# Graph layer with relation weights: statistics of three node blocks moved to ScalarE, the first line's cell columns to VectorE, scatters and first-edge loads reordered

## The chip, the cores and the metric

One core of one Trainium2 chip runs the whole program. The metric is device time in microseconds (us) of one execution. The core has TensorE (PE, matmuls), VectorE (DVE), ScalarE (ACT), GpSimd (POOL) and SyncE (SP, which issues most plain DMAs). Each engine executes its own queue strictly in order and waits there on semaphores of others. GpSimd issues the indirect DMAs (gathers and scatters); in the profile such a DMA keeps POOL busy for about a microsecond.

## The reference

```python
h = relu(layernorm(x))                         # x: 625 x 512
for r in range(4):                             # 20625 edges, sorted by dst
    total_msg += (h[src] @ W_rel[r] + b_rel[r]) * where(edge_type == r, edge_weight, 0)[:, None]
agg = segment_sum(total_msg, dst) / maximum(segment_sum(edge_weight, dst), 1)[:, None]
x1  = layer_norm(h + h @ W_self + b_self + agg, ln1_g, ln1_b)
out = x + layer_norm(x1 + gelu(x1 @ W_ffn1 + b_ffn1) @ W_ffn2 + b_ffn2, ln2_g, ln2_b)
```

## The kernel before

The 625 nodes lie in NB = 5 blocks of up to 128 rows. The program has three stages.

**Table stage.** For each of the R = 4 relations and each block, one step (20 steps, `step = r * NB + i`) multiplies the normalised block with the relation's weights (`table_rows`, L463), VectorE adds the bias and scales the rows (L476), and SP stores them in a DRAM table of 4 x 640 rows. A message of an edge is then one row of that table times the edge's weight. `pre_norm` prepares a block: mean and variance on VectorE (L437, L439), `z = relu(x - mean)` on VectorE for blocks 0 to 2 (L427) and on ScalarE for blocks 3 and 4 (L424), and `(var + eps) ** -0.5` on GpSimd (`rsqrt_pow`, L399), which `table_rows` uses as the rows' scale. PE then transposes z (L406) and ScalarE copies the result (L412). During the first relation, the transposes of block i + 1 stand between the second and third matmul of block i.

In the same 20 steps the edges are prepared. The edges of the first and last node block are not gathered by row: GpSimd scatters their weights into a matrix of "cells" in DRAM (L746), 46 columns of 128 edges each, in two "lines" (31 columns of block 0, 15 of block 4). `line_columns` computes keys and places for a whole line, `line_sums` (L732 to L740) then handles a piece of up to 8 columns on VectorE, and each column becomes one `scatter`: an indirect DMA and a small memset (L749). `load_sums` brings a finished cell matrix back to SBUF; chunk sums (L1485) multiply it with the table. For the inner blocks, `first_edges` finds on PE and VectorE the first edge group of each node (`x_group`, L906), GpSimd loads three tiles of them (`x_edges`, L910), and `first_rows` on VectorE turns these into table rows. Tuples such as `COLUMNS_AT` say at which step each of these parts is written.

**Edge stage.** GpSimd gathers 102 tiles of 128 table rows (L1308, three of them at L1386), each into one of 10 buffers `ms`. ScalarE and VectorE weigh or add them and split them into a high and a low part (`eh`, `el`), and PE sums them by node with one-hot matrices (L1369). Chunk sums, self parts (L501), layer norms and the feed-forward products (L1054, L1074) of finished blocks fill the other engines. The order of this stage is written out as a list of operation numbers, `ORDER`, which was fitted beforehand with a model of durations and due times; each engine then runs it in order. The first gather stands behind a small memset that waits until all but the last table row block are stored (`after_stores`, L761).

**Tail.** The last block's sums, norm, feed-forward and store.

Of the kernel before, what the change touches and what calls it, by code (L numbers as in the profile page):

```python
# [16 lines left out]
P = 128  # L17
# [7 lines left out]
class EdgePlan:  # L25
# [176 lines left out]
def gnn_layer(ctx, tc, x, edges, edge_line, edge_groups, w_self, w_rel, w_ffn1, w_ffn2, rows_in, bf_in, out, n_edges):  # L202
# [218 lines left out]
    def pre_norm(i, mean):  # L421
        if i > 2:
            nc.scalar.activation(rx[:, i, 2:3], mean, AF.Copy, scale=-1.0)
            nc.scalar.activation(z[:, i, :], xs[:, i, :], AF.Relu, bias=rx[:, i, 2:3])  # L424
        else:
            for c in (slice(0, D // 2), slice(D // 2, D)) if i == 0 else (slice(0, D),):
                nc.vector.tensor_scalar(z[:, i, c], xs[:, i, c], mean, 0.0, op0=ALU.subtract, op1=ALU.max)  # L427
# [752 lines left out]
    with tc.manual_schedule(engines={PE, DVE, ACT, mybir.EngineType.Pool}):  # L1180
# [12 lines left out]
        for r in range(R):  # L1193
            for i in range(NB):
# [8 lines left out]
                if step + 3 < NB:  # L1203
                    pre_norm(step + 3, x_stats(step + 3))
# [560 lines left out]
```

## Time and profile before

| | us |
|---|---|
| median of 3 runs | 260.82 (260.43 to 260.83) |
| the profiled execution, its own time | 259.69 |
| its span | 257.8 |
| busy: PE, DVE, POOL, ACT | 241.5, 198.6, 169.3, 106.4 |

The profiled execution is 1.13 us faster than the median of the runs, and 1.9 us of its time lie outside the span. A timeline row reads: start, duration, engine, line, operation, output <- inputs, and in square brackets how long the engine had been idle before it and what ended that. `x4` is a merged run of four; a 128 x 512 float32 matmul appears as two records, so the four matmuls of a step give eight.

### The profile page before, as it was taken

To read this page: it belongs to the slowest core of one execution; us is meant where nothing else is said; L and a number is where in the kernel's file an instruction comes from. 1 tells how busy PE (TensorE), PEld (TensorE's weight loads), DVE (VectorE), ACT (ScalarE), POOL (GpSimd) and SP (SyncE) were. 2 spreads that over 40 slices of the span, in tenths; PEclk is the share of its full clock that TensorE was granted. 3 is DMA by queue.
4 is the path that set the end of the run, shared out by engine and by line. 5 is a ranking of instruction groups with operands and counts; after the bars stand their busy time and mean duration, and the time that the engine had idled before them with its cause. 6 is when DMAs were issued, how large, how long until landed. Compare 5 with 4: busy or idle time off the path is not lost.

```text
span 257.8 us, 3594 instructions
## 1 busy us (share of the span) xinstructions
PE 241.5 (94%) x1051; PEld 141.5 (55%) x1051; DVE 198.6 (77%) x474; ACT 106.4 (41%) x328; POOL 169.3 (66%) x230
## 2 busy tenths in 40 slices
PE   8899999999999958899999999999999999999980
PEld 6334444344455623455544466657966759549660
DVE  2787799998999750999867999898887897764344
ACT  3036600000231011876544655695666664606420
POOL 5487888688875867777777777778777777410000
PEclk9999999999999995999999999999999999999997
DMA  6999999983371149979889998776777677501021
GB/s 188 334 396 410 383 368 368 299 328 133 95 275 43 45 135 402 355 211 336 256 285 354 367 342 267 214 215 188 207 211 214 213 218 215 182 0 43 0 84 40
DMA packets 23997, 59.44 MB, mean 231 GB/s; under 512 B 4419, under 2 KB 8743, under 8 KB 22822
## 3 DMA queue, kind: packets, MB, share of 16 engines
q0 software_dynamic: 9728, 26.79, 33.6%
q1 hardware_dynamic: 13920, 30.91, 33.3%
q10 hardware_dynamic: 326, 1.48, 1.6%
q8 instruction: 9, 0.15, 0.2%
q14 instruction: 14, 0.11, 0.1%
HBM read 49.99 MB, written 9.17 MB: 229 GB/s over the span
## 4 chain that ended last, share of the span: by engine, by line
PE 64%; DVE 13%; DMA 10%; ACT 4%; POOL 4%; issue 3%; SPq 1%; POOLq 0%; DVEq 0%
PE ps L463 16%; PE ps L1054 11%; PE ps L1074 11%; PE acc L1485 10%; PE acc L1369 8%; PE ps L501 4%; DMA tr<-table 3%; DMA line<-in_edge_line_dram 2%; DMA out_dram<-ow 2%; DMA ms<-table,row_i 2%; POOL cells L746 2%; POOL x_edges L910 1%; DVE ow L1099 1%; PE ps L673 1%; PE ps L406 1%
## 5 line engine op out<-in xcount | busy, mean ns | idle before, releaser
L1308 POOL DMA_INDIRECT ms<-table,row_i x99 | 97.1, 981 | 31.2 <-issue 16.0
L463 PE MATMUL ps<-wr,T 128*128 128x512 f32 (+2 forms) x168 | 71.3, 577 | 0.8 <-ACT T L412 0.8
L746 POOL DMA_INDIRECT cells<-weight,cell x46 | 47.7, 1036 | 10.7 <-issue 6.4
L463 PEld LDWEIGHTS ps<-wr,T 128*128 128x128 f32 x168 | 30.4, 190 | 35.7 <-issue 29.2
L1344 DVE SCALAR_TENSOR_TENSOR add<-ms,wgt_g,add 128x512 f32<-128x512 f32 x55 | 40.4, 749 | 6.7 <-ACT add L1314 3.5
L1054 PEld LDWEIGHTS ps<-T,w_sb 128*128 128x128 f32 x320 | 39.2, 191 | 5.9 <-issue 3.3
L1054 PE MATMUL ps<-T,w_sb 128*128 128x128 f32 (+2 forms) x320 | 39.8, 275 | 0.5 <-ACT T L1548 0.4
L1074 PE MATMUL ps<-w_sb,gT 128*128 128x512 f32 (+2 forms) x96 | 36.5, 523 | 0.3 <-ACT gT L1060 0.3
L1485 PE MATMUL acc<-tr,sums_w 128*128 128x512 f32 x60 | 31.2, 623 | 0.5 <-DMA tr<-table 0.5
L1314 ACT ACTIVATE add<-ms,wgt_g 128x512 f32<-128x512 f32 x30 | 20.6, 688 | 10.7 <-DVE el L1322 8.9
L1074 PEld LDWEIGHTS ps<-w_sb,gT 128*128 128x128 f32 x96 | 16.6, 190 | 13.6 <-issue 9.3
L1318 ACT CAST eh<-add 128x512 fp32r<-128x512 f32 x25 | 14.5, 583 | 15.1 <-DVE add L1344 14.0
L1322 DVE TENSOR_TENSOR el<-add,eh 128x512 fp32r<-128x512 f32 x25 | 17.0, 683 | 3.4 <-ACT eh L1318 1.8
L1369 PE MATMUL acc<-eh,oh 128*128 128x512 f32 x34 | 16.3, 511 | 3.3 <-ACT eh L1332 3.3
L501 PE MATMUL ps<-ws_sb,T 128*128 128x512 f32 x40 | 18.6, 592 | 0.0
L659 ACT ACTIVATE ohw<-os,w 128x128 fp32r<-128x128 f32 x34 | 10.7, 389 | 18.0 <-DVE os L641 18.0
L1060 ACT ACTIVATE gT<-ps,bf 128x128 f32<-128x128 f32 (+1 forms) x40 | 13.6, 359 | 11.0 <-PE ps L1054 10.6
L1369 PE MATMUL acc<-el,oh 128*128 128x512 f32 x34 | 16.7, 516 | 1.2 <-DVE el L1336 0.7
L1485 PEld LDWEIGHTS acc<-tr,sums_w 128*128 128x128 f32 x60 | 10.8, 194 | 8.1 <-issue 5.5
L1332 ACT ACTIVATE eh<-ms,ed 128x512 fp32r<-128x512 f32 x9 | 6.2, 712 | 21.1 <-DMA tr<-table 15.8
L476 DVE SCALAR_TENSOR_TENSOR tr<-ps,rx,brel_bc 128x512 f32<-128x512 f32 x15 | 11.1, 743 | 4.8 <-PE ps L463 4.8
L1336 DVE SCALAR_TENSOR_TENSOR el<-ms,ed,eh 128x512 fp32r<-128x512 f32 x9 | 6.6, 747 | 9.1 <-ACT eh L1332 9.1
(250 smaller groups left out, 314.8 us busy)
## 6 DMA issues: line engine op xcount, KB each, us to landing
tr<-table SPq DMA_DIRECT2D x11, 512.0 KB, 5.8
w_sb<-in_L_gnn_W_ffn_dram SPq DMA_DIRECT2D x2, 2048.0 KB, 10.0
table<-tr SPq DMA_DIRECT2D x15, 256.0 KB, 4.4
wr<-in_L_gnn_W_rel_dram SPq DMA_DIRECT2D x3, 1024.0 KB, 7.8
cells<-zeros SPq DMA_DIRECT2D x2, 1280.0 KB, 10.8
ms<-table,row_i POOLq DMA_INDIRECT x99, 3.9
rows<-in_rows_dram SPq DMA_DIRECT2D x1, 1280.0 KB, 12.7
sums_w<-cells ACTq DMA_DIRECT2D x1, 1280.0 KB
```

What stands on the lines that cost most here:

```text
L463: nc.tensor.matmul(p_[:, :h.stop - h.start], hT[i][:, k, :], wr_sb[r][:, k, h], start=(k == 0), stop=(k == KD - 1))
L501: nc.tensor.matmul(p[0], hT[i][:, k, :], ws_sb[:, k, :], start=(k == 0), stop=(k == KD - 1))
L746: s = nc.gpsimd.indirect_dma_start(out=cells[i][:, :], out_offset=bass.IndirectOffsetOnAxis(ap=cell[i][:, k:k + 1], axis=0), in_=weight[i] ...
L1054: nc.tensor.matmul(pu[:, low:nn + first], w1_sb[:, k, f * P:(f + 1) * P], x1T_b()[:, k, low:nn + first], start=(k == 0), stop=(k == KD - 1))
L1074: nc.tensor.matmul(po[h][:n, :w], box["gT"][:, f, at], w2_sb[:, f, c], start=(f == 0), stop=(f == KF - 1))
L1308: nc.gpsimd.indirect_dma_start(out=ms[j], out_offset=None, in_=table[:, :], in_offset=bass.IndirectOffsetOnAxis(ap=row_i[:, j:j + 1], axis=0))
L1314: nc.scalar.activation(box["sum"], ms[j], AF.Copy, scale=wgt_g[:, (j - GROUP0) // EG, 0:1])
L1318: nc.scalar.copy(box["high"], box["sum"])
L1322: nc.vector.tensor_sub(box["low"], box["sum"], box["high"].bitcast(F32))
L1344: nc.vector.scalar_tensor_tensor(to, ms[j], wgt_g[:, k, q:q + 1], box["sum"], op0=ALU.mult, op1=ALU.add)
L1369: nc.tensor.matmul(acc[bs], w.bitcast(F32) if of.dtype == F32 else w, of, start=first, stop=last)
L1485: nc.tensor.matmul(acc[b,], sums_w[b][:, c, :], kept[(b, c) if (b, c) in kept else c], start=first, stop=last)
```

## The change

1. Blocks 2, 3 and 4 are normalised on ScalarE. `centre_x` sums the row with the accumulator of a Copy, turns the sum into the negative mean, and writes z; `spread_x` sums the squares of `x - mean` in the same way and makes `var + eps`. Both write a scrap tile `junk` in PSUM. `centre_x` of blocks 2, 3, 4 comes at steps 0, 1, 2, `spread_x` with GpSimd's power at steps 1, 2, 3 (before, VectorE did blocks 0, 1, 2 ahead of the steps and 3, 4 in steps 0 and 1).
2. `line_columns` of the first line runs on VectorE, not on GpSimd, and has 10 operations behind the key where it had 12. `place` is now multiplied by `found` once for a line; so each piece of `line_sums` has one operation less.
3. Pieces come at steps 0, 1, 4, 7, 10, 11, 13 (before 0, 2, 4, 7, 10, 12, 14). Scatters are written as soon as their piece is there, two per step in steps 0 to 2; before, five were kept back once the pieces were done and were written behind the loads of the first edges.
4. Of the preparations, one-hot matrices, self weights, limits, degrees, `rows` and the load of line 0's cells move by one to three steps, as the tuples show. `x_group` stays at step 17.
5. The edge stage has a new `ORDER`; the model's entries that made it are `CELLS`, which went from 3.0 to 1.5, and `FIRSTS = 5.0`, a due time for `first_rows`.

```diff
 ORDER = [
-    398, 400, 403, 408, 440, 441, 401, 7, 22, 0, 402, 404, 24, 2, 407, 23, 25, 29, 8, 3, 409, 1, 442, 34, 39, 443,
+    0, 401, 404, 409, 399, 402, 23, 25, 3, 403, 441, 8, 24, 1, 30, 412, 405, 35, 4, 408, 413, 26, 400, 410, 442, 443,
...
     def pre_norm(i, mean):
-        if i > 2:
-            nc.scalar.activation(rx[:, i, 2:3], mean, AF.Copy, scale=-1.0)
-            nc.scalar.activation(z[:, i, :], xs[:, i, :], AF.Relu, bias=rx[:, i, 2:3])
-        else:
-            for c in (slice(0, D // 2), slice(D // 2, D)) if i == 0 else (slice(0, D),):
-                nc.vector.tensor_scalar(z[:, i, c], xs[:, i, c], mean, 0.0, op0=ALU.subtract, op1=ALU.max)
+        for c in (slice(0, D // 2), slice(D // 2, D)) if i == 0 else (slice(0, D),):
+            nc.vector.tensor_scalar(z[:, i, c], xs[:, i, c], mean, 0.0, op0=ALU.subtract, op1=ALU.max)
         nc.vector.tensor_scalar(rx[:, i, 0:1], var_of[i], EPS, None, op0=ALU.add)
         rsqrt_pow(rx[:, i, :])
+
+    junk = ps_acc.tile([P, D], F32, tag="acc", name="junk")
+
+    def centre_x(i):
+        nc.scalar.activation(junk, xs[:, i, :], AF.Copy, accum_out=rx[:, i, 0:1])
+        nc.scalar.activation(rx[:, i, 2:3], rx[:, i, 0:1], AF.Copy, scale=-1.0 / D)
+        nc.scalar.activation(z[:, i, :], xs[:, i, :], AF.Relu, bias=rx[:, i, 2:3])
+
+    def spread_x(i):
+        nc.scalar.activation(junk, xs[:, i, :], AF.Square, bias=rx[:, i, 2:3], accum_out=rx[:, i, 0:1])
+        nc.scalar.activation(rx[:, i, 0:1], rx[:, i, 0:1], AF.Copy, scale=1.0 / D, bias=EPS)
...
     def line_columns(i, e):
-        e.tensor_scalar(ok, d[:, own], float(b * P), None, op0=ALU.is_ge)
+        e.tensor_scalar(part, s[:, own], 0.5 - P / 2, 1.0 / P, op0=ALU.add, op1=ALU.mult)
         e.tensor_scalar(at, d[:, own], float(b * P + P), None, op0=ALU.is_lt)
...
+        e.tensor_add(to, to, at)
+        e.tensor_mul(to, to, ok)
...
     def line_sums(i, k0, k1):
-        nc.vector.scalar_tensor_tensor(earlier, earlier, 0.0, found[i][:, at], op0=ALU.is_equal, op1=ALU.mult)
-        nc.vector.tensor_mul(earlier, earlier, place[i][:, at])
+        nc.vector.scalar_tensor_tensor(earlier, earlier, 0.0, place[i][:, at], op0=ALU.is_equal, op1=ALU.mult)
...
-    HOTS_AT, SELF_AT, ADDS_AT = (15, 16, 17), 15, (16, 17, 18)
+    HOTS_AT, SELF_AT, ADDS_AT = (13, 14, 16), 13, (15, 17, 18)
-    BEHIND = 5
-    CELLS = 3.0
+    CELLS, FIRSTS = 1.5, 5.0
-    COLUMNS_AT, LINE_AT, DEGREE_HOTS_AT = (0, 2, 4, 7, 10, 12, 14), 9, (8, 9)
-    COLUMNS_OF_EDGES_AT, LOAD_AT, LIMITS_AT = 5, 16, (3, 6)
-    DEGREES_AT, SPREAD_AT, FIRST_AT, OUTER_HOTS_AT = 13, 15, 17, (17, 18)
+    COLUMNS_AT, LINE_AT, DEGREE_HOTS_AT = (0, 1, 4, 7, 10, 11, 13), 8, (9, 12)
+    COLUMNS_OF_EDGES_AT, GROUPS_AT, LOAD_AT, LIMITS_AT = 5, 6, 15, (4, 6)
+    DEGREES_AT, SPREAD_AT, FIRST_AT, OUTER_HOTS_AT = 14, 16, 17, (15, 16)
+    NORM_AT, ROOT_AT = ((0, 2), (1, 3), (2, 4)), ((1, 2), (2, 3), (3, 4))
...
-        line_columns(0, nc.gpsimd)
-        pre_norm(2, x_stats(2))
+        line_columns(0, nc.vector)
...
-                if step + 3 < NB:
-                    pre_norm(step + 3, x_stats(step + 3))
+                if step in dict(NORM_AT):
+                    centre_x(dict(NORM_AT)[step])
+                if step in dict(ROOT_AT):
+                    spread_x(dict(ROOT_AT)[step])
+                    rsqrt_pow(rx[:, dict(ROOT_AT)[step], :])
...
-                while len(columns) > (BEHIND if not pieces and step <= FIRST_AT else 0):
+                for _ in range(2 if step < 3 else len(columns)):
                     scatter(*columns.pop(0))
...
                 if step == FIRST_AT:
                     first_edges()
                     load_first_edges()
-                    while columns:
-                        scatter(*columns.pop(0))
...
-    rows_of_first = op("DVE", 2.2, first_rows, rank=(0.3,), level=0.2)
+    rows_of_first = op("DVE", 2.2, first_rows, after=[op("cells", FIRSTS, None)], rank=(0.3,), level=0.2)
```

Three places of the queues matter below. The first is GpSimd's queue between the scatters of the last line (`cells`) and the first gather (`ms`). Before:

```order
L746 DMA cells_101<-weight_180,cell_181 329600x1
L749 MEMSET idle 128x32
L910 DMA x_edges<-in_edge_groups_dram,x_group 128x12 x3
L746 DMA cells_101<-weight_180,cell_181 329600x1
L749 MEMSET idle 128x32
...
L761 MEMSET idle 128x2
L1308 DMA ms_879<-table,row_i 128x512
```

The part left out is four more pairs of scatter and memset. Now:

```order
L750 DMA cells_101<-weight_181,cell_182 329600x1
L753 MEMSET idle 128x32
L914 DMA x_edges<-in_edge_groups_dram,x_group 128x12 x3
L765 MEMSET idle 128x2
L1312 DMA ms_864<-table,row_i 128x512
```

The five scatters that stood between the three loads of first edges and the gathers stand ahead of those loads.

The second is ScalarE's queue from the copy of block 1's transposes (`T_153`) to that of block 3's (`T_155`). Before:

```order
L412 COPY T_153<-ps_78 128x4x128
L423 ACTIVATE rx<-mv_x_305 128x1
L424 ACTIVATE z<-xs,rx 128x512
L412 COPY T_154<-ps_80 128x4x128
L423 ACTIVATE rx<-mv_x_342 128x1
L424 ACTIVATE z<-xs,rx 128x512
L412 COPY T_155<-ps_78 128x4x128
```

Now:

```order
L412 COPY T_153<-ps_78 128x4x128
L430 ACTIVATE junk,rx<-xs 128x512
L431 ACTIVATE rx<-rx 128x1
L432 ACTIVATE z<-xs,rx 128x512
L412 COPY T_154<-ps_80 128x4x128
L430 ACTIVATE junk,rx<-xs 128x512
L431 ACTIVATE rx<-rx 128x1
L432 ACTIVATE z<-xs,rx 128x512
L435 ACTIVATE junk,rx<-xs,rx 128x512
L436 ACTIVATE rx<-rx 128x1
L412 COPY T_155<-ps_78 128x4x128
```

Ahead of each copy there are now the sum, mean and z of the next block but no wait for VectorE's statistics, and from the second on the squares of the block before.

The third is SP's queue behind the last table rows (`m`). Before:

```order
L478 DMA table<-m_869 128x128
L1480 DMA tr_0_1051<-table 128x512
L1480 DMA tr_1_1094<-table 128x2x512
L765 DMA sums_w_186<-cells_101 128x2560
L1480 DMA tr_3_1164<-table 128x2x512
```

Now:

```order
L485 DMA table<-m_854 128x128
L769 DMA sums_w_187<-cells_101 128x2560
L1484 DMA tr_0_1019<-table 128x512
L1484 DMA tr_1_1042<-table 128x2x512
L1484 DMA tr_3_1132<-table 128x2x512
```

The load of block 4's cells, which waits for the last scatters, now stands ahead of the first loads of table rows for the chunk sums.

More of the change, by code (lines that the diff above doesn't have):

```diff
@@ L705, in line_columns @@
         near, ok, to = 1.5 * 2.0 ** 23, found[i], place[i]
-        e.tensor_scalar(ok, d[:, own], float(b * P), None, op0=ALU.is_ge)
+        e.tensor_scalar(part, s[:, own], 0.5 - P / 2, 1.0 / P, op0=ALU.add, op1=ALU.mult)
         e.tensor_scalar(at, d[:, own], float(b * P + P), None, op0=ALU.is_lt)
-        e.tensor_mul(ok, ok, at)
-        e.tensor_scalar(part, s[:, own], 0.5 - P / 2, 1.0 / P, op0=ALU.add, op1=ALU.mult)
         e.tensor_scalar(part, part, near, None, op0=ALU.add)
+        e.scalar_tensor_tensor(to, s[:, own], float(NC * P - 1), t[:, own], op0=ALU.mult, op1=ALU.add)
         e.tensor_scalar(part, part, -near, None, op0=ALU.add)
-        e.tensor_scalar(to, s[:, own], float(NC * P - 1), None, op0=ALU.mult)
-        e.tensor_add(to, to, d[:, own])
-        e.tensor_add(to, to, t[:, own])
-        e.tensor_scalar(part, part, float(P - P * NC * P), float(-b * P), op0=ALU.mult, op1=ALU.add)
-        e.tensor_sub(part, part, spill[i])
-        e.tensor_add(to, to, part)
+        e.scalar_tensor_tensor(ok, d[:, own], float(b * P), at, op0=ALU.is_ge, op1=ALU.mult)
+        e.scalar_tensor_tensor(at, d[:, own], float(-b * P), spill[i], op0=ALU.add, op1=ALU.subtract)
+        e.scalar_tensor_tensor(to, part, float(P - P * NC * P), to, op0=ALU.mult, op1=ALU.add)
+        e.tensor_add(to, to, at)
+        e.tensor_mul(to, to, ok)
     def line_check(i):
@@ L1217, in gnn_layer @@
                     edge_columns()
-                if step == COLUMNS_OF_EDGES_AT + 1:
+                if step == GROUPS_AT:
                     group_columns()
```

58 rows, old and new, of the table ORDER are left out of this document.

## The prediction

> **What bounds the kernel now.** I read the page's groups first, then the chain that ended last, GpSimd's timeline, and then PE's, VectorE's and SyncE's timelines around the places where GpSimd waits. The groups, and one row of the chain:
>
> ```profile
> L1308 POOL DMA_INDIRECT ms<-table,row_i x99 | 97.1, 981 | 31.2 <-issue 16.0
> L746 POOL DMA_INDIRECT cells<-weight,cell x46 | 47.7, 1036 | 10.7 <-issue 6.4
> ```
>
> ```profile
> 22.26 29.18 PE ps L463 x68
> ```
>
> The chain runs over PE, which is busy for 94% of the span, so it looks as if PE set the time. GpSimd's timeline says otherwise. Its rows (start, duration, work, in brackets the idle time before and its releaser):
>
> ```profile
> 45.57 0.15 POOL L749 MEMSET idle<- 128x32 bf16 x1
> 47.66 0.96 POOL L746 DMA_INDIRECT cells<-weight,cell  x1 [1.94 <-DVE weight L740]
> ...
> 75.76 0.15 POOL L749 MEMSET idle<- 128x32 bf16 x1
> 79.28 1.21 POOL L910 DMA_INDIRECT x_edges<-in_edge_groups_dram,x_group  x1 [3.37 <-DVE x_group L906]
> ...
> 84.04 1.00 POOL L746 DMA_INDIRECT cells<-weight,cell  x1 [0.30 <-issue]
> ...
> 90.14 0.14 POOL L749 MEMSET idle<- 128x32 bf16 x1
> 90.34 0.10 POOL L761 MEMSET idle<- 128x2 bf16 x1
> 91.78 1.07 POOL L1308 DMA_INDIRECT ms<-table,row_i  x1 [1.34 <-issue]
> ...
> 140.13 0.95 POOL L1308 DMA_INDIRECT ms<-table,row_i  x1 [0.30 <-issue]
> 141.38 0.95 POOL L1308 DMA_INDIRECT ms<-table,row_i  x1 [0.30 <-issue]
> ...
> 221.59 0.95 POOL L1308 DMA_INDIRECT ms<-table,row_i  x1 [0.30 <-DVE add L1344]
> ```
>
> From 91.78 to 221.59 stand 102 gathers, one every 1.25 us (140.13 to 141.38). 101 such steps are 126.25 us; the stretch takes 129.81. So gathers run back to back from their first to their last, and behind the last one follows work that cannot begin sooner:
>
> ```profile
> 228.07 0.75 DVE L489 SCALAR_TENSOR_TENSOR z<-acc,rdeg,z 128x512 f32<-128x512 f32 x1 [1.85 <-PE acc L1369]
> ```
>
> The norm and feed-forward of the last sums take from there to the span's end at 257.8. PE's many busy rows ahead of it are work that is spread over the gathers' time. So the end follows the first gather: a microsecond earlier there is one at the end, as long as the consumers keep up. What stands ahead of it on GpSimd is 46 scatters, three loads and a memset, with two waits of size, 1.94 us for a piece of `line_sums` and 3.37 us for `x_group`. Between 47.66 and 75.91 it goes from scatter to scatter.
>
> **The change, part by part.** First the front on PE, where ScalarE takes over the statistics:
>
> ```profile
> 12.57 0.62 PE L406 MATMUL ps<-ident,z 128*128 128x128 f32 x4
> 13.03 1.88 PE L463 MATMUL ps<-wr,T 128*128 128x512 f32 x4
> 15.54 1.98 PE L463 MATMUL ps<-wr,T 128*128 128x512 f32 x4 [0.63 <-ACT T L412]
> ...
> 17.80 1.88 PE L463 MATMUL ps<-wr,T 128*128 128x512 f32 x4
> 19.84 1.98 PE L463 MATMUL ps<-wr,T 128*128 128x512 f32 x4 [0.16 <-ACT T L412]
> ...
> 22.10 29.35 PE L463 MATMUL ps<-wr,T 128*128 128x512 f32 x68
> ```
>
> ```profile
> 14.06 0.20 ACT L423 ACTIVATE rx<-mv_x 128x1 f32<-128x1 f32 x1 [4.14 <-DVE mv_x L439]
> 14.30 0.72 ACT L424 ACTIVATE z<-xs,rx 128x512 f32<-128x512 f32 x1
> ```
>
> In the chain 68 records take 29.18 us, 0.429 each, so a group of four takes 1.72. From 12.57 to 22.10, 9.53 us, PE has four such groups and three groups of transposes of 0.46 (12.57 to 13.03): 6.88 + 1.38 = 8.26. It loses 1.27 us, because ScalarE makes z only when VectorE's statistics are there, at 14.06 after 4.14 us idle. With the sums on ScalarE that wait goes. It then makes two long passes (sum and squares) and two short ones more per block: 0.72 + 0.72 + 0.20 + 0.20 = 1.84 us. One block's turn becomes 0.20 + 0.72 + 0.56 (copy of T) + 1.84 = 3.3 us beside PE's 1.72 x 2 + 0.46 = 3.9, so 0.6 us are free. No row shows a pass with an accumulator; VectorE's accumulator reads take 0.08. Bounds: the whole 1.27 is won, or every one of three such turns is 0.72 us longer than costed, 2.16 in all against 1.27, a loss of 0.9. I take a gain of 1.1, near the first, since the turn has room.
>
> Second, VectorE. Its pieces pay one short operation less, and the first line's ten operations are new there. The same twelve operations of the second line are there already:
>
> ```profile
> 22.62 0.20 DVE L736 TENSOR_TENSOR earlier<-earlier,place 128x8 f32<-128x8 f32 x1
> ...
> 51.09 0.21 DVE L706 TENSOR_SCALAR found<-line_f 128x15 f32<-128x15 f32 x1
> ...
> 52.88 0.23 DVE L717 TENSOR_TENSOR place<-place,line_s 128x15 f32<-128x15 f32 x1
> ```
>
> Twelve took 2.0 us, so ten take 1.7. The three blocks' statistics, 1.4 + 1.0 + 1.0 us by their starts and ends, leave VectorE in the same stretch; the two cancel at least, and I count nothing. The pieces up to the fourth bring 2 x 0.20 = 0.4 us on the way to the scatter at 47.66, which waits for VectorE. VectorE is full from 27.5 to there, after a wait for PE. So that scatter comes 1.1 + 0.4 = 1.5 us sooner, at 46.2. GpSimd is free at 45.7 and has no more to do than now: its twelve column operations are gone, and of the powers there are as many as before. From there to the 41st scatter all stand back to back.
>
> Third, `x_group`. At 75.91 GpSimd is done with 41 scatters and waits 3.37 us; then come the loads (79.28 to 84.04, 4.76 us), and the five scatters (84.04 to 90.34, 6.30 us) after them. Now the five stand ahead of the loads. 46 scatters end at 75.91 - 1.5 + 6.30 = 80.7. If `x_group` is ready by then, the whole wait is gone: 3.37.
>
> ```profile
> 75.30 1.56 DVE L840 TENSOR_TENSOR sums_w<-rel,row_w 128x1368 bf16<-128x1368 bf16 x1
> ...
> 78.85 0.15 DVE L906 TENSOR_SCALAR x_group<-ps 128x3 int32<-128x3 f32 x1
> ```
>
> Of the two `sums_w` products of 1.56 us one stands ahead of `x_group` now and both do then; so at 78.85 + 1.56 - 1.5 = 78.9 plus 0.15 it is there, 1.7 us ahead of need. If the work moved ahead of it costs more than that, the wait returns in part; if all 3.37 return, the gain is 1.5. I take 3.4.
>
> Fourth, the memset and the first gather. Both stay with 0.10 and the 1.34 us of issue. The last stores of the table must have landed before the memset; five scatters fewer stand between the loads and it, so less covers them. GpSimd would reach it at 80.7 + 4.76 = 85.5, and SyncE's last store is issued by 84.88 (75.40 + 9.48):
>
> ```profile
> 75.40 9.48 SPq L478 DMA_DIRECT2D table<-m  x4
> 92.00 2.09 SPq L1480 DMA_DIRECT2D tr<-table  x2
> 94.82 0.32 SPq L765 DMA_DIRECT2D sums_w<-cells  x1
> ```
>
> The memset leaves the last block's store out, so it waits for an earlier one. The 1.34 may shrink to the 0.30 seen between gathers (a gain of 1.04). I keep it.
>
> Sum: 1.1 + 0.4 + 3.4 = 4.9 us. The first gather would start at 86.9, where it was at 91.78. Against the profiled execution's 259.69 this makes 254.8; that execution is 1.13 us below the median of the runs, and against 260.82 it makes **255.9**, my forecast. The largest gain in the sum is 1.27 + 0.4 + 3.4 + 1.04 = 6.1, to 254.7, or 253.6 on the profiled execution.
>
> **Can PE follow?** For this the gaps and the granted clock of PE behind the first gather:
>
> ```profile
> 96.27 0.50 PE L1369 MATMUL acc<-eh,oh 128*128 128x512 f32 x1 [2.58 <-ACT eh L1332]
> ...
> 99.20 0.80 PE L1369 MATMUL acc<-eh,oh 128*128 128x512 f32 x1 [0.76 <-ACT eh L1332]
> ...
> 109.11 0.50 PE L1369 MATMUL acc<-el,oh 128*128 128x512 f32 x1 [0.65 <-DVE el L1336]
> ```
>
> ```profile
> 90.00:95.00 5.00, 3.69 (x11) 1.42 (x9) 3.22 (x9) 0.00 (x0) 3.00 (x6) 1.00 0.34 106
> 95.00:100.00 5.00, 2.97 (x7) 1.43 (x8) 0.75 (x1) 1.91 (x3) 3.78 (x5) 0.72 0.93 336
> 100.00:105.00 5.00, 5.00 (x13) 2.22 (x12) 1.57 (x3) 2.32 (x7) 3.78 (x5) 0.60 1.00 385
> ```
>
> PE waits 2.58 + 0.76 + 0.65 = 4.0 us there, and at a clock of 0.72 and 0.60 (the third figure from a row's end) it loses 0.28 x 5 + 0.40 x 5 = 3.4 us more. Gathers that come 4.9 us sooner close these gaps, so PE has up to 7.4 us to give, and 4.9 are asked. The clock fell after a gap of 2.58 us; with the gap gone I expect it to stay up. The Trainium skill, "TensorE: Matmul & The Clock Gate", section "What's actually happening", says that the clock goes to half after an idle window of about 3.4 us. The trace does not agree in size: the gap is shorter, and the fall came all the same. By that rule no fall would be expected with shorter gaps, and the sum stays 255.9; by the trace, a gap of some 2 us left over is enough, and then the first rival's 257.5 holds.
>
> **Rivals.** *PE becomes the bound.* If the clock falls again, PE can only give the gaps that wait for ScalarE's first tiles, 2.58 + 0.76 = 3.3: 260.82 - 3.3 = 257.5. For it: PE is busy for 94%. Against: from 90.00 to 93.69, where the gap of 2.58 us begins, PE is busy without a break (3.69 us in the row of 90 to 95), so first tiles that come 4.9 us sooner find it at work.
>
> *The front is lost.* The powers for blocks 2 to 4 stand on GpSimd behind two scatters each, 2 x 1.27 = 2.5 us; VectorE, in order, would wait for the row scale with the pieces behind it. If one such delay reaches the fourth piece, the gain of 1.5 is gone and 2.5 are added: 3.4 - 2.5 = 0.9, hence 259.9. Against: VectorE takes the scale only after PE's product, some 4 us behind z.
>
> *Slower.* SyncE's load of block 4's cells stands ahead of the first loads of table rows and waits for the last scatter. The sizes (KB each, us to landing) and, last, the landing of the scatters:
>
> ```profile
> tr<-table SPq DMA_DIRECT2D x11, 512.0 KB, 5.8
> cells<-zeros SPq DMA_DIRECT2D x2, 1280.0 KB, 10.8
> ```
>
> ```profile
> DMA to landing us min/median/max: 2.2/5.6/11.9
> ```
>
> The last scatter, issued at 79.4, lands at 85.0 at the median and at 91.3 at the latest. The cells are 1280 KB and may take the 10.8 us of the row of that size, with tr's 5.8 behind them: at worst 91.3 + 0.3 + 10.8 + 5.8 = 108.2. In the new order PE first needs that tile between the third and fourth gathered one, which land about 95, so with its other work at some 99. A wait of 9.2 us against 7.4 to give makes 260.82 + 1.8 = 262.6, and 266.0 if the 3.4 of the clock does not come back either. It decides from a landing at 106.4, or 103.0 with the clock lost. Against: at the median the tile lands at 101.9 even with no overlap of the two transfers, and before, the load at 94.82 stood 5.6 us behind its scatter at 89.18.
>
> *No change*: the gathers' own irregularity (129.81 - 126.25 = 3.6) could grow by 4.9 us as they now meet the cells' load; no row speaks for it.
>
> **How the numbers follow.** A change of 0.2%, 0.5 us, is about what a measurement of this kernel can tell from none. Forecast 0.55 (its own range 254.7, the largest sum, to 258.0, with 2.1 us of `x_group`'s wait or of the accumulators left); PE the bound 0.17; front lost 0.09, of it a third within 0.2%; no change 0.03; slower 0.14; still faster than all 0.02. Faster: 0.55 + 0.17 + 0.06 + 0.02 = 0.80; same 0.06; slower 0.14. The range 253.6 to 260.0 goes from the largest sum to the front lost and leaves out the slower case and little else.
>
> **What would show it.** In the profile after: no wait of PE for T between 12 and 22; the fourth piece's first scatter at about 46.2; 46 scatters on end, loads of first edges at about 80.8 with no idle time for `x_group` ahead of them; the first gather at about 86.9, gathers 1.25 us apart, the last at about 216.7 and `z` at about 223.2; a granted clock near 1.00 from 90 to 105. It would be wrong if GpSimd waited for VectorE's pieces or `x_group` as long as now, if PE waited in the chunk sums for tr, or if gaps of PE and a low clock turned up after the first gather.

## The result, and the profile after

The changed kernel takes 257.48 us (median of 4 runs, 256.29 to 257.89), the kernel before 260.62 on the same chip; the ratio is 0.9874, with a 95% interval of 0.9837 to 0.9911. That is 3.1 us less, where 4.9 were forecast, and inside the range. Its profiled execution has a span of 255.8 us, against 257.8.

GpSimd's timeline of the changed kernel, at the places that the prediction named (line numbers are those of the changed file: the scatters are L750, the loads L914, the gathers L1312):

```profile
17.42 1.71 POOL L750 DMA_INDIRECT cells<-weight,cell  x1 [8.21 <-DVE tr L483]
...
47.56 0.96 POOL L750 DMA_INDIRECT cells<-weight,cell  x1 [0.17 <-issue]
...
68.88 4.04 POOL L750 DMA_INDIRECT cells<-weight,cell  x1 [0.17 <-issue]
72.92 0.14 POOL L753 MEMSET idle<- 128x32 bf16 x1
73.22 2.18 POOL L750 DMA_INDIRECT cells<-weight,cell  x1 [0.17 <-issue]
...
84.67 0.96 POOL L750 DMA_INDIRECT cells<-weight,cell  x1 [0.17 <-issue]
85.63 0.14 POOL L753 MEMSET idle<- 128x32 bf16 x1
85.94 1.00 POOL L914 DMA_INDIRECT x_edges<-in_edge_groups_dram,x_group  x1 [0.17 <-issue]
...
89.77 0.95 POOL L1312 DMA_INDIRECT ms<-table,row_i  x1 [0.19 <-issue]
...
221.80 1.33 POOL L1312 DMA_INDIRECT ms<-table,row_i  x1 [0.30 <-issue]
```

All three waits are gone: scatters and loads stand end to end from 17.42 to 89.77. But the first gather starts at 89.77 and not at 86.9. Two scatters of 4.04 and 2.18 us stand in the row, where others take 0.96, and the fourth piece's first scatter (47.56) has hardly moved. The page's group of all 46 scatters says the same:

```profile
L750 POOL DMA_INDIRECT cells<-weight,cell x46 | 52.8, 1148 | 15.5 <-DVE tr L483 8.2
```

From the first scatter to the first gather, by these rows and those of before:

| us | before | after | difference |
|---|---|---|---|
| waits for pieces and `x_group` (1.46 at 24.63, 1.94, 3.37) | 6.77 | 0 | -6.77 |
| the 46 scatters' own time | 47.7 | 52.8 | +5.1 |
| loads of first edges, and last memset to first gather | 4.76 + 1.50 | 3.83 | -2.43 |
| the rest (powers, small memsets, issue), by difference | 13.88 | 15.72 | +1.84 |
| sum | 74.61 | 72.35 | -2.26 |

The prediction had as many powers as before on GpSimd's way to the fourth piece. In number that holds for the whole queue, but the powers of blocks 2 and 3 ran ahead of the first scatter before (at 15.53) and stand between scatters now. A scatter behind one starts 0.70 us after the memset ahead of it ends (20.76 to 21.46), where 0.17 is usual; so two of them cost about 1.1 of the 1.84.

The first scatter itself starts 0.25 us later, which leaves 2.01 for the first gather. What VectorE did beside the two long scatters:

```profile
68.71 1.56 DVE L844 TENSOR_TENSOR sums_w<-rel,row_w 128x1368 bf16<-128x1368 bf16 x1
70.20 1.28 DVE L1235 TENSOR_TENSOR xs<-xs,rows 128x512 f32<-128x512 f32 x2
71.40 0.68 DVE L1245 TENSOR_TENSOR rows<-rows,bf_bc 128x512 f32<-128x512 f32 x1
72.00 0.73 DVE L483 SCALAR_TENSOR_TENSOR m<-ps,rx,brel_bc 128x512 f32<-128x512 f32 x1
72.67 1.56 DVE L844 TENSOR_TENSOR sums_w<-rel,row_w 128x1368 bf16<-128x1368 bf16 x1
```

From 68.71 to 72.08 run products and additions whose operands all lie in SBUF, without a break; the scatter that began at 68.88 ends at 72.92, 0.84 after them. Before, the first of the two products ran at 75.30 to 76.86, while GpSimd stood idle for `x_group` (75.91 to 79.28). The wait that the change removes had hidden this work.

The second half of the result is a surprise. In these two executions the last gather stands at the same place (221.59 and 221.80), since the stretch of 102 gathers took 132.03 us and not 129.81. The 2.0 us of the span came behind it. VectorE at the end, before:

```profile
239.19 0.75 DVE L1094 SCALAR_TENSOR_TENSOR ow<-ow,mv_y,rows 128x512 f32<-128x512 f32 x1 [3.84 <-DMA out_dram<-ow]
...
250.02 0.56 DVE L1084 TENSOR_TENSOR ow<-ps,z 128x384 f32<-128x384 f32 x1 [2.20 <-DMA out_dram<-ow]
```

and after:

```profile
228.23 0.75 DVE L496 SCALAR_TENSOR_TENSOR z<-acc,rdeg,z 128x512 f32<-128x512 f32 x1 [0.56 <-PE acc L1373]
...
235.30 1.42 DVE L1098 SCALAR_TENSOR_TENSOR ow<-ow,mv_y,rows 128x512 f32<-128x512 f32 x2 [0.78 <-DMA out_dram<-ow]
...
246.53 0.56 DVE L1088 TENSOR_TENSOR ow<-ps,z 128x384 f32<-128x384 f32 x1 [2.13 <-PE ps L1078]
```

From the last norm's `z` to the span's end it took 29.7 us (228.07 to 257.8), and takes 27.6 (228.23 to 255.8). Before, VectorE waited 3.84 and 2.20 us until an output store had left a buffer `ow`; in the new order the first wait is 0.78, and the second one is for PE.

### The profile page after: what moved, and what is told of

Same layout as the page of the kernel before. It is cut to its first block, busy times and chain, and to the rows that moved or that the text cites. A ratio compares the mean times of both kernels' runs of the same rounds, so it can differ in the third digit from the quotient of the medians.

```text
span 255.8 us, 3608 instructions
## 1 busy us (share of the span) xinstructions
PE 240.3 (94%) x1051; PEld 141.9 (55%) x1051; DVE 196.8 (77%) x466; ACT 112.2 (44%) x345; POOL 171.5 (67%) x218
## 4 chain that ended last, share of the span: by engine, by line
PE 35%; DVE 31%; issue 12%; POOL 8%; DMA 8%; ACT 2%; SPq 1%; DVEq 0%; POOLq 0%; ACTq 0%
PE ps L1058 8%; PE acc L1489 7%; PE ps L1078 6%; PE acc L1373 5%; POOL ms L1312 4%; PE ps L508 4%; DVE tr L483 4%; PE ps L470 3%; DVE z L496 3%; POOL cells L750 3%; DMA line<-in_edge_line_dram 3%; DMA ms<-table,row_i 3%; DVE add L1348 3%; DMA x_edges<-in_edge_groups_dram,x_group 2%; DVE same L737 2%
## 5 line engine op out<-in xcount | busy, mean ns | idle before, releaser
L1312 POOL DMA_INDIRECT ms<-table,row_i x99 | 99.6, 1006 | 30.2 <-issue 14.8
L470 PE MATMUL ps<-wr,T 128*128 128x512 f32 (+2 forms) x168 | 72.6, 587 | 0.5 <-DMA wr<-in_L_gnn_W_rel_dram 0.5
L750 POOL DMA_INDIRECT cells<-weight,cell x46 | 52.8, 1148 | 15.5 <-DVE tr L483 8.2
L470 PEld LDWEIGHTS ps<-wr,T 128*128 128x128 f32 x168 | 31.3, 194 | 35.7 <-issue 31.9
L1058 PEld LDWEIGHTS ps<-T,w_sb 128*128 128x128 f32 x320 | 38.5, 192 | 5.4 <-issue 1.7
L1489 PE MATMUL acc<-tr,sums_w 128*128 128x512 f32 x60 | 29.3, 595 | 0.0
L1373 PE MATMUL acc<-eh,oh 128*128 128x512 f32 x34 | 18.0, 544 | 1.9 <-ACT eh L1336 1.4
L1373 PE MATMUL acc<-el,oh 128*128 128x512 f32 x34 | 17.5, 538 | 0.2 <-DVE el L1340 0.2
L483 DVE SCALAR_TENSOR_TENSOR tr<-ps,rx,brel_bc 128x512 f32<-128x512 f32 x15 | 11.2, 745 | 5.6 <-POOL rx L399 5.6
L508 PEld LDWEIGHTS ps<-ws_sb,T 128*128 128x128 f32 x40 | 7.4, 190 | 7.1 <-issue 6.9
L1373 PEld LDWEIGHTS acc<-eh,oh 128*128 128x128 f32 x34 | 6.5, 190 | 7.4 <-issue 3.3
```

The source lines that it names most:

```text
L470: nc.tensor.matmul(p_[:, :h.stop - h.start], hT[i][:, k, :], wr_sb[r][:, k, h], start=(k == 0), stop=(k == KD - 1))
L483: made_row.append(nc.vector.scalar_tensor_tensor(m[:, h], p_[:, :h.stop - h.start], rx[:, i, 1:2], brel_bc[:, r * D + h.start:r * D + h.st ...
L508: nc.tensor.matmul(p[0], hT[i][:, k, :], ws_sb[:, k, :], start=(k == 0), stop=(k == KD - 1))
L750: s = nc.gpsimd.indirect_dma_start(out=cells[i][:, :], out_offset=bass.IndirectOffsetOnAxis(ap=cell[i][:, k:k + 1], axis=0), in_=weight[i] ...
L1058: nc.tensor.matmul(pu[:, low:nn + first], w1_sb[:, k, f * P:(f + 1) * P], x1T_b()[:, k, low:nn + first], start=(k == 0), stop=(k == KD - 1))
L1312: nc.gpsimd.indirect_dma_start(out=ms[j], out_offset=None, in_=table[:, :], in_offset=bass.IndirectOffsetOnAxis(ap=row_i[:, j:j + 1], axis=0))
```

## The experiments

Two theories explain the 3.1 us. The *gather theory* is the prediction's: the end follows the first gather, and the front made it 2.0 us earlier. The *tail theory*: the new order of the edge stage saved 2 us behind the last gather. A third one, *PE*, is the prediction's first rival, which gave just the measured time, 257.5. For the front, the *collision theory* says that VectorE's long operations hold up GpSimd's scatters. One table for all runs, from their traces (the stretch is from the first gather's start to the last one's; the tail from the last `z` to the span's end), with the ratio to the kernel before on the same chip; runs on different chips are compared by these ratios:

| kernel | first gather | stretch | tail | ratio, 95% interval |
|---|---|---|---|---|
| before | 91.78 | 129.81 | 29.7 | 1 |
| changed | 89.77 | 132.03 | 27.6 | 0.9874 (0.9837 to 0.9911) |
| e1: changed, old order | 89.03 | 131.30 | 30.0 | 0.9929 (0.9905 to 0.9954) |
| e2: before, new order | 92.88 | 131.43 | 27.8 | 0.9974 (0.9949 to 0.9999) |
| e3: products later | 89.18 | 130.78 | 27.8 | 0.9838 (0.9807 to 0.9869) |
| e4: before, gathers late | 94.68 | 131.57 | 30.0 | 1.0154 (1.0120 to 1.0189) |
| e5: products, additions left out | 85.77 | 132.08 | 27.6 | 0.9703 (0.9641 to 0.9766) |
| e6: roots on VectorE | 90.40 | 133.10 | 27.8 | 0.9848 (0.9760 to 0.9937) |
| e7: before, five `ow` | 91.71 | 131.51 | 27.0 | 0.9895 (0.9833 to 0.9957) |
| e8: five scatters behind | 90.89 | 131.93 | 27.5 | 0.9879 (0.9816 to 0.9941) |
| e11: products on ScalarE | 87.39 | 132.86 | 27.9 | 0.9767 (0.9718 to 0.9816) |
| e12: and additions apart | 86.48 | 132.31 | 27.6 | 0.9796 (0.9752 to 0.9839) |

**The two halves apart (e1, e2).** The two kernels exchange their `ORDER`:

```diff
 e1, in the changed kernel
-ORDER = [0, 401, 404, ...]
+ORDER = [0] + [n + 1 for n in order of before]
 e2, in the kernel before
-ORDER = [398, 400, 403, ...]
+ORDER = [n - 1 for n in order of the change if n]
```

> The changed kernel with the edge-stage order of before (its numbers shifted by the one new entry, which stands first); the table stage stays as changed. Gather theory (the end follows the first gather, as predicted): first gather at about 89.8, 2.0 us sooner than before's 91.78, time 260.6 - 2.0 = 258.6, ratio 0.992. Tail theory (the 2 us of the span came behind the last gather, where before VectorE waited 3.84 and 2.20 us for output stores, and the new order of the edge stage is what changed there): those waits come back, time 260.3 to 260.9, ratio 0.999 to 1.001.

> The kernel before with the edge-stage order of the change (numbers shifted by one); statistics, cells, scatters and loads of first edges as before. Gather theory: first gather stays at 91.8, so the time stays: 260.6, ratio 1.000. Tail theory: first gather at 91.8, but from the last norm of sums to the end 27.6 us instead of 29.7: 258.5, ratio 0.992.

Both theories are half right. The front alone (e1) brings 0.71% (258.61 against 260.75) with a tail of 30.0 us, and its wait for the store is back:

```profile
248.21 0.56 DVE L1085 TENSOR_TENSOR ow<-ps,z 128x384 f32<-128x384 f32 x1 [2.18 <-DMA out_dram<-ow]
```

The order alone (e2) has a tail of 27.8 us with the front of before, but its ratio is 0.9974 (259.76), so at most half of the 2 us shows in the time. Two things are on record for the rest: its profiled execution began its scatters 1.1 us later than before's, and 2.18 us of its runs lie outside the span, where it is 1.82 before. Whether they are the whole reason stays open. The ratios multiplied are 0.9903, within the interval of the whole change. e2 missed what either theory had given for it (260.6 or 258.5).

**Does the end follow the first gather? (e4)**

```diff
     def after_stores():
+        for _ in range(5):
+            nc.gpsimd.memset(own_buffers["ms"][-1], 0.0)
         wait_for(nc.gpsimd.memset(idle[:, :2], 0.0), stored[:NC - 1], "rows are stored")
```

> The kernel before with five memsets of a 128 x 512 buffer on GpSimd ahead of the first gather, some 2 to 4 us (the trace gives the delay d). Gather theory: the time rises by d, to 262.6 to 264.6. PE theory (the end is the sum of PE's work and PE has to give only what its gaps are): PE already waits for the first gathered tiles, so nearly all of d is lost too unless later slack takes it; a rise of under half of d would speak for slack behind the gathers and against the gather theory.

The first gather started 2.90 us later, the time rose by 3.45 (260.75 to 264.20). By the expectation a rise of this size fits both theories, so PE's rows have to tell them apart. PE waits 9.68 us for the first tiles and its clock is at 0.50:

```profile
103.80 0.80 PE L1371 MATMUL acc<-eh,oh 128*128 128x512 f32 x1 [9.68 <-ACT eh L1334]
```

```profile
95.00:100.00 5.00, 0.00 (x0) 0.00 (x0) 0.00 (x0) 0.00 (x0) 3.78 (x5) 0.68 0.81 297
100.00:105.00 5.00, 1.20 (x4) 1.11 (x5) 0.75 (x1) 1.50 (x3) 3.78 (x5) 0.50 1.00 377
```

From the start to 120 PE is busy for 107.0 us, where it was 113.0 before, and it comes back to a lower clock (0.50 and 0.80 in the ten microseconds from 100 on, where it was 0.60 and 1.00). Had the end been the sum of PE's work, these 6 us would have come back there; the time rose by little more than the gathers' own delay. So the gathers set the end, and PE has time to spare behind them.

The table says the same without e4: over the eight kernels with the new order the first gather goes from 85.77 (e5) to 92.88 (e2), 7.1 us, and the ratio from 0.9703 to 0.9974, which is 7.1 us too; two pairs of neighbours stand the other way round.

**The long scatters (e3, e5).** e3 puts the products back to the steps where they stood before; e5 leaves them and the additions out:

```diff
 e3
-    DEGREES_AT, SPREAD_AT, FIRST_AT, OUTER_HOTS_AT = 14, 16, 17, (15, 16)
+    DEGREES_AT, SPREAD_AT, FIRST_AT, OUTER_HOTS_AT = 14, 16, 17, (17, 18)
 e5
         line_columns(0, nc.vector)
+        nc.gpsimd.memset(outer_hots, 0.0)
...
-                    degree_hots(j0, nj, outer_hots[:, j0 - GROUPS:j0 - GROUPS + nj, :])
+                    pass
-                        nc.vector.tensor_add(xs[:, b, :], xs[:, b, :], b2_bc)
+                        pass
-                    nc.vector.tensor_add(b1_bc, b1_bc, bf2_bc)
```

> The changed kernel with the two large sums_w products of VectorE (1.56 us each) back at steps 17 and 18, from 15 and 16. In the changed kernel two scatters beside them took 4.04 and 2.18 us where others take 0.96. Collision theory (VectorE's product holds GpSimd up): those two fall to 1.0 to 1.3 us, the last scatter starts 3 to 4 us sooner, the first gather at about 86 to 87, and if the end follows the first gather the time is 254 to 255; PE's wait of 2.10 us for counts goes too. If the long scatters have nothing to do with the products, first gather 89.8 and 257.5. If PE and not the gathers sets the end, first gather 86 to 87 and 256.5 to 257.5.

> The changed kernel without VectorE's long operations beside the last scatters: the two sums_w products of the outer degrees (1.56 us each), the five additions of the feed-forward bias to xs and the one to rows (0.6 us each) are left out; a GpSimd memset before the first scatter clears what the products would have written. Collision theory (a scatter is held up while VectorE runs such operations on SBUF): the scatters of 4.04 and 2.18 us fall to 1.0 to 1.4, the first gather comes 3.5 to 4.5 us sooner than 89.8, at about 86, and with the end following it the time is 253.2 to 254.2 (ratio 0.972 to 0.975). Otherwise (their length comes from the stores or the queue): still one of over 2 us, first gather 89 to 90, and 256 to 257.5 for PE's wait of 2.10 us for the counts, which goes in any case.

e3 refuted the simple form: instead of two long scatters there were three, each beside such operations, and the first gather came only 0.6 us sooner. GpSimd's scatters and VectorE's products and additions, in e3:

```profile
68.41 2.55 POOL L750 DMA_INDIRECT cells<-weight,cell  x1 [0.16 <-issue]
...
73.80 2.24 POOL L750 DMA_INDIRECT cells<-weight,cell  x1 [0.17 <-DVE m L483]
...
78.88 2.35 POOL L750 DMA_INDIRECT cells<-weight,cell  x1 [0.17 <-issue]
```

```profile
68.24 1.28 DVE L1235 TENSOR_TENSOR xs<-xs,rows 128x512 f32<-128x512 f32 x2
...
73.62 1.57 DVE L844 TENSOR_TENSOR sums_w<-rel,row_w 128x1368 bf16<-128x1368 bf16 x1
...
78.82 1.57 DVE L844 TENSOR_TENSOR sums_w<-rel,row_w 128x1368 bf16<-128x1368 bf16 x1
```

So e3 exchanged collisions for others; its ratio lies within the interval of the changed kernel's. It also bears on PE, which had a gap of 4.92 us and a clock of 0.50 there, where the changed kernel has a gap of 1.43 and a clock of 1.00:

```profile
97.58 0.80 PE L1373 MATMUL acc<-eh,oh 128*128 128x512 f32 x1 [4.92 <-ACT eh L1336]
```

```profile
95.00:100.00 5.00, 2.42 (x3) 0.83 (x3) 4.69 (x25) 4.36 (x12) 3.78 (x5) 0.50 1.04 396
```

To 120 PE is busy 0.9 us less than in the changed kernel (111.9 and 112.8), with a lower clock from 90 to 120 (0.89 and 1.00), and e3 is not slower for it (256.30): again PE does not set the end.

In e5, which leaves the work out, no scatter from 60 on is over 1.3 us, all 46 have 48.08 us, and the first gather is at 85.77, 4.0 us sooner. The time is 253.94. By the ratios that is 4.5 us less than the changed kernel, with the two intervals up to some 2 us either way; the times themselves, from two chips, are 3.5 apart. Both halves of the expectation held: the collision costs about 4 us, and the end follows.

**Powers and moved scatters (e6, e8).** e6 computes the three powers on VectorE by nine short operations (a guess by shifts, three Newton steps, a scaling); e8 writes the five scatters behind the loads again:

```diff
 e6
-                    rsqrt_pow(rx[:, dict(ROOT_AT)[step], :])
+                    root_x(dict(ROOT_AT)[step])
 e8
-                for _ in range(2 if step < 3 else len(columns)):
+                for _ in range(2 if step < 3 else len(columns) - (0 if pieces or step > FIRST_AT else 5)):
                     scatter(*columns.pop(0))
...
                     load_first_edges()
+                    while columns:
+                        scatter(*columns.pop(0))
```

> The changed kernel with the power (var + eps) ** -0.5 of blocks 2, 3 and 4 computed by nine short operations on VectorE and not by GpSimd between the scatters. In the changed kernel the three powers take 0.77 us each of GpSimd's path (2.3 in all) and VectorE waits 0.82, 2.40 and 2.41 us for them; nine operations of some 0.19 are 1.7 per block. If the powers are what lost the front: scatters stand 2.3 us closer, first gather at 87.0 to 87.8, time 255.0 to 255.8, ratio 0.980. If VectorE's pieces then come too late or the long scatters only move: first gather 88.5 to 89.8, time 256.3 to 257.6.

> The changed kernel with the last five scatters written behind the loads of first edges again, as before. By the prediction (moving them fills the wait of 3.37 us for x_group): first gather 3.4 us later than 89.8, time 260.9. By the trace of the changed kernel (GpSimd is done with 41 scatters at about 79.3, x_group is there at 78.4, so there is no wait to fill any more): first gather 89.3 to 90.3, time 257.0 to 258.0, and the moved scatters gain nothing by themselves.

In the changed kernel VectorE waits for the powers, which stand on GpSimd behind two scatters each:

```profile
21.32 0.75 DVE L483 SCALAR_TENSOR_TENSOR tr<-ps,rx,brel_bc 128x512 f32<-128x512 f32 x1 [0.82 <-POOL rx L399]
24.48 0.75 DVE L483 SCALAR_TENSOR_TENSOR tr<-ps,rx,brel_bc 128x512 f32<-128x512 f32 x1 [2.40 <-POOL rx L399]
27.64 0.75 DVE L483 SCALAR_TENSOR_TENSOR tr<-ps,rx,brel_bc 128x512 f32<-128x512 f32 x1 [2.41 <-POOL rx L399]
```

In e6 these waits are gone, and the third of these rows still starts at 27.65: the nine operations take as long as the waits did, so e6 does not show what the waits' removal alone would bring. GpSimd, quicker now, waits for VectorE's fourth piece instead:

```profile
47.53 0.97 POOL L760 DMA_INDIRECT cells<-weight,cell  x1 [1.74 <-DVE weight L754]
```

So the first gather did not gain (90.40), as the expectation's second branch had it, though it came later than its 89.8, and the time is 0.5 above that branch's 257.6. e8 has no wait for `x_group` either, although the five scatters stand behind the loads; its first gather is 1.1 us later (90.89; 0.36 of it is a later first scatter), and its ratio is that of the changed kernel. Moving the scatters did not bring the 3.4 us.

**The stores at the end (e7).**

```diff
-    HOTS = 8
+    HOTS = 4
-    OW = 4
+    OW = 5
```

> The kernel before with five buffers ow for the output norms, where it has four (the small tiles of the norms have four buffers in place of eight, to make room). Tail theory: VectorE's waits of 3.84 and 2.20 us for output stores go, and from the last norm of sums to the end it takes 27.2 to 28.2 us, where it took 29.7: time 258.5 to 259.3, ratio 0.992 to 0.995. If the stores only fill time in which PE works anyway: 260.4 to 261.0.

With one more `ow` the kernel before has a tail of 27.0 us and 0.9895: the wait of 2.20 is gone, one of 3.13 is left at 240.11. Its ratio is even below the 0.992 expected. So a fifth buffer gives the old order as much as the new order saves behind the gathers (27.6 us from `z` to the end), which speaks for the waits for stores as the cause there too.

**A faster version (e9 to e12).** ScalarE has no work from 30 to 65. The products go there, complete; e10 and e12 also take the additions apart:

```diff
+    def outer_degree_hots():
+        for j in range(ND - GROUPS):
+            nc.scalar.activation(outer_hots[:, j, :], row_w, AF.Square, bias=rel_f[:, j:j + 1], scale=-1.0)
+        nc.scalar.activation(outer_hots, outer_hots, AF.Relu, bias=1.0, scale=-1.0)
...
-    DEGREES_AT, SPREAD_AT, FIRST_AT, OUTER_HOTS_AT = 14, 16, 17, (15, 16)
+    DEGREES_AT, SPREAD_AT, FIRST_AT, OUTER_HOTS_AT = 14, 16, 17, (8,)
 e10, e12 also
-    HOTS_AT, SELF_AT, ADDS_AT = (13, 14, 16), 13, (15, 17, 18)
+    HOTS_AT, SELF_AT, ADDS_AT = (13, 14, 16), 13, (12, 14, 15, 16, 18)
```

> The changed kernel, complete, with the two sums_w products moved from VectorE to ScalarE, which is idle from about 30 to 65: 72 short passes (row_w - rel) squared and one pass relu(1 - .), some 10 us there. The additions to xs and rows stay on VectorE. Collision theory: the scatter of 4.04 us falls to about 2.5 (the additions alone, as in the run with the products at 17 and 18), the one of 2.18 us to about 1; no scatter beside the products on ScalarE grows; first gather at 86.5 to 87.5, time 254.3 to 255.3 (ratio 0.975 to 0.980). If ScalarE's passes hold up GpSimd as VectorE's do, the scatters between 41 and 52 grow instead and the first gather stays at 89 to 90, 257 to 258.

> As the run before, and the five additions of the bias to xs stand one per step at steps 12, 14, 15, 16 and 18, where they stand in pairs at 15, 17 and 18. Collision theory, with a run of such operations costing what it lasts beyond a scatter's own slack: one addition of 0.65 us holds a scatter up by 0 to 0.4, a pair by 1 to 1.5; first gather another 0.5 to 1.5 us sooner, at 85.5 to 86.5, time 253.5 to 254.6. If only the sum of VectorE's time counts: no further gain, 254.3 to 255.3.

e9 and e10 ran on a chip where the kernel before took 306.99 us; their ratios are 0.9597 and 0.9717. Their first gathers are at 98.64 and 101.95, and PE's rows have long waits for "issue" (ten of 0.5 to 1.9 us between 63 and 74 in e9, one of 11.26 at 83.50 in e10). Their times can't be set beside the others, so e11 and e12 are the same two kernels on another chip.

> The kernel with the products on ScalarE once more, since the kernel before took 307 us in the last comparison and not 260 to 261, so that its trace can't be set beside the others. Collision theory as there: the scatter of 4.04 us at about 2.5, that of 2.18 at about 1, first gather at 86.5 to 87.5, time 254.3 to 255.3, ratio 0.975 to 0.980. If ScalarE's passes hold up GpSimd too, or the pieces of VectorE set the scatters' pace by then: first gather 88.5 to 90, ratio 0.984 to 0.988.

> The kernel with the products on ScalarE and the additions one per step once more, for the same reason. Collision theory: another 0.5 to 1.5 us sooner than the run beside it, first gather at 85.5 to 86.5, ratio 0.971 to 0.977. If only the sum of VectorE's time counts: the same as the run beside it within 0.3%.

e11 takes 255.62 us (before: 261.33), ratio 0.9767, and beats both kernels. ScalarE's passes, and the longest scatter that is left:

```profile
41.16 15.69 ACT L851 ACTIVATE sums_w<-row_w,rel_f 128x38 bf16<-128x38 bf16 x72 [10.65 <-DVE rel_f L811]
56.88 2.48 ACT L852 ACTIVATE sums_w<-sums_w 128x2736 bf16<-128x2736 bf16 x1
```

```profile
68.95 2.54 POOL L750 DMA_INDIRECT cells<-weight,cell  x1 [0.17 <-issue]
```

The passes take 18.2 us and not the 10 expected, but PE reads their result only at 82.4. The first gather is at 87.39 and the longest scatter 2.54 us, beside three additions, as expected; the ratio is in the range given, the time 0.3 above it. In e12, with the additions apart, the longest one from 60 on is 1.35 and the first gather another 0.9 sooner, as the collision theory had it, but the ratio (0.9796) missed its 0.971 to 0.977, and the time is that of e11 (255.77), as the other branch had it. Whether that 0.9 is real in the time stays open.

## Why the prediction was right, and where not, by its own steps

- **That the end follows the first gather** held: 2.90 us of delay cost 3.45 (e4), 4.0 us won brought some 4.5 by the ratios (e5). With PE 94% busy, its gaps behind the first gather were slack.
- **The front on PE** (1.1): PE's waits for T between 13 and 22 did go, and one block's turn on ScalarE is as costed, with the accumulator's read at 0.19. From the third block's transposes to the end of the fifth's it is 1.35 us shorter (13.25 to 21.43, where it was 12.57 to 22.10), but half of that was lost ahead of it, and the rest behind it: it reached nothing. **The pieces** (0.4): also not. The fourth piece's first scatter came at 47.56, for 47.66: of 1.5 us 0.1 was left. This is the second rival's mechanism, the powers behind two scatters each, at the size that eats the gain but adds nothing; VectorE starts its full stretch at 27.64 where it was 27.52. The step that failed is "VectorE is full from 27.5 to there, after a wait for PE": the wait for PE became a wait for GpSimd. What the front gains without that wait is not known: e6 puts work of the same length in its place.
- **The wait for `x_group`** (3.4): it went, and `x_group` was written at 78.23, somewhat ahead of the 79.1 worked out. But the 26 scatters from the fourth piece on, costed at the pace of before, took 38.2 us (47.56 to 85.77) where the same 26 took 34.5 before (47.66 to 75.91 and 84.04 to 90.28). 3.7 us were given back, since VectorE's products now met scatters and not an idle GpSimd. That is the mis-sized term: a wait was counted as empty time, with no look at what else ran in it.
- **The loads and the 1.34 us ahead of the first gather**, which I kept, fell by 2.4 us together: the third load had been 1.68 beside a product, and the issue is 0.19. This is beyond the bound that I gave (1.04 for the issue alone).
- **"Work that cannot begin sooner"** was wrong of the tail: the new order made it 2.1 us shorter (e2, e1, e7). I had read the last gather and not the two waits for stores behind it.
- **The gathers' pace**: before's profiled execution has the shortest stretch of all (129.81); three other runs of the old order have 131.3 to 131.6, those of the new order 130.8 to 133.1. That is the likely reason why the spans of the two profiles (2.0 us apart) show less than the times (3.1).
- **PE as the bound** gave 257.5 and so the measured time, by chance: its condition, a clock that falls again, was not met (from 85 to 115 the granted clock stayed at 1.00, as forecast), and e3, e4 and e5 speak against its mechanism. **The slower case** did not come: PE waits for no tile of tr between 90 and 120; cells were loaded from 88.09 on.

So 255.9 was 1.6 too low: the front brought 2.9 us less than summed, the tail 2.1 more, and the stretch took some 0.6 longer than in those three runs (less than such stretches differ among themselves), which makes 2.9 - 2.1 + 0.6 = 1.4. That the forecast came so near is in good part luck: the tail, which it did not have, made up for most of what the front lost.

## What to carry to other kernels

A wait that is removed is worth its length only if nothing hid in it: list what the other engines run in that time and what those operations do to the engine that now works through it. Look for such rows by duration: an operation that takes 4 us where most of its 45 likes take 1 points to a neighbour. And read the chain behind the last step of the bound as well; a buffer too few there cost as much as the whole front gave.

## What the runs showed of the hardware

Indirect DMAs of GpSimd are held up while VectorE runs operations on two tensors that both lie in SBUF: 4.04 us beside a run of 3.4 us, 2.2 to 2.6 beside 1.9 to 2.8, 0.96 alone; 18.2 us of ScalarE's passes over the same data did nothing of the kind (e11). Nor did an operation with one of its tensors in PSUM (L483 from 47.06 to 47.80 in the changed kernel, with a scatter of 0.96 at 47.56). It matters which begins first. A scatter that begins while such an operation runs ends about 0.84 us after it (72.92 after 72.08; in e3 70.96 after 70.12), or after one in the middle of the run (in e3 76.04, 0.85 after the product, with additions still running to 76.40). One that began just ahead of two additions was not held up, in the changed kernel:

```profile
76.98 0.96 POOL L750 DMA_INDIRECT cells<-weight,cell  x1 [0.17 <-issue]
```

```profile
77.00 1.31 DVE L1235 TENSOR_TENSOR xs<-xs,rows 128x512 f32<-128x512 f32 x2
```

The Trainium skill, "SBUF — State Buffer", section "Who interferes with whom", has a VectorE instruction with two inputs in SBUF contend with GpSimd's reads. It also tells of an older probe in which `tensor_tensor` did not stall a DMA, and infers why. The first half agrees with these rows; the second does not: additions and comparisons of that kind held up scatters here.

PE's granted clock fell behind a shorter gap than the 2.58 us of before: it is 0.76 in 75 to 80 of the changed kernel, behind this wait of 2.10 us, and stayed at 1.00 behind the 1.43 us at 98.76:

```profile
75.62 0.39 PE L906 MATMUL ps<-counts,before 128*128 128x3 f32 x2 [2.10 <-DVE counts L975]
```

```profile
75.00:80.00 5.00, 4.38 (x15) 2.58 (x16) 4.64 (x24) 0.87 (x3) 4.34 (x9) 0.76 0.20 66
```
